# The product with C moved ahead of lane X's VectorE operations in the odd steps of a conv, state-space scan and attention kernel

## Chip, cores and metric

The kernel runs on one core of one Trainium2 chip. The metric is the device time of one execution in microseconds. The time before is the median of three runs, 5233.21 us (5232.01 to 5235.14).

## What is computed

The input is x, four images of 128 channels and 64 x 64 pixels, in fp32. Two layers follow each other. Layer 0 is a convolution block with a selective state-space scan ("mamba"); layer 1 is attention over the 4096 tokens of an image, followed by a mixture of eight experts of which each token takes two. Cut to what matters here:

```python
xn  = ln(group_norm(x));  y = xn + fc2(gelu(ln(conv3x3_depthwise(xn))))
u   = ln(y) split into 4 chunks of 32 channels           # each chunk is a sequence of 4096
xin = silu(conv1d(in_proj(u)));  z = silu(in_proj'(u))
dt, B, C = split(xin @ x_proj.T);  delta = softplus(dt @ dt_proj.T + b)
h_t = exp(delta_t * A) * h_(t-1) + delta_t * B_t * xin_t   # 64 channels x 16 states
y_t = sum over the 16 states of h_t * C_t                  # the product with C
m   = ((y + D * xin) * z) @ out_proj.T + chunks
t   = x + ln(xn + m) @ proj.T;  t = t + attention(ln(t));  out = t + experts(ln(t))
```

## The kernel before

**Work and tiles.** An image is cut into 8 blocks of 512 tokens, so there are 32 blocks (b, i). For a block the scan is done for two halves of the channels (p = 0, 1) and for the 16 states in pairs (n = 0, 2, ... 14): 512 units `(b, i, p, n)` in all (line 1299). The main loop (lines 1322 to 1373) gives each unit two steps of a counter `slot`, an even and an odd one, hence 1024 steps; a step takes some 4 to 5 us in the long middle of the run. Attention, the convolution block and the experts are threaded through the same steps.

**What a step issues, in this order.** `fetch` issues SyncE's load of the rows of B or C that a later unit needs (`rows`, a ring of 4 buffers); `prepared` has ScalarE make a decay `da` (and, in odd steps, copy the carried state into the next `h`). In an even step `driven` multiplies `h <- rows, du` on VectorE. Then `summed_up`, when a half block is done. Then `advance("X", True)`: the second half of lane X's current stage. Then `next(groups)` issues the score matmuls `sc` of attention on TensorE and `exponentials` two exponentials `pT <- sc` on ScalarE. In an even step `scan` follows on VectorE (`h <- da, state, h`, 1025 elements per partition), in an odd step `read`: the product with C, `hc <- rows, h`. Then come `advance("Y", False)`, the matmuls `y <- ident, hc` that TensorE uses to turn and sum the halves of an `hc`, `advance("Y", True)`, `kept` (ScalarE saves the state), the matmuls `av <- pT, v` of the group before, and last `advance("X", False)`.

**Order is fixed.** Every operation goes through `Queue` (lines 461 to 471), whose helper (line 467 in the profile, for all of them) ties it to the one before it on its engine. So each engine runs its operations in the order in which the Python code emits them, and only waits for others come on top.

**Lanes.** X and Y are two queues of stages, each written as a generator. A stage's first half (`advance(lane, False)`) mostly issues TensorE work into the lane's one PSUM tile (`ps_X`, `ps_Y`); its second half (`advance(lane, True)`, in the step after for lane X) reads that tile, mostly on VectorE. Lane Y prepares blocks (`first_norm`, `conv`, `inputs`). Lane X closes blocks (`closed`, line 848: the output projection, two layer norms, q, k and v) and, when the softmax sums of a pair of blocks are there, finishes them (`finished`, line 1087: router and experts).

**GpSimd in the layer norms.** `normalised` (line 545) takes mean and variance on VectorE (`st`, `mv`), then writes `rs` and `shift` there, and has GpSimd raise `rs` to the power -0.5 (`rs <- rs, mhalf`) and multiply `shift <- shift, rs`. One stage later ScalarE applies both (`xt`), ahead of that step's exponentials in ScalarE's queue.

**The product's own ties.** `hc` has two buffers, and is read by TensorE no sooner than the step after (`due`, lines 1348 to 1350: slot + 1 and slot + 2, two later when n is 0). It reads `h`, which the scan of the step before has written, and a `rows` buffer, which SyncE can fill again once the product is done.

Of the kernel before, what the change touches and what calls it, by code (L numbers as in the profile page):

```python
# [36 lines left out]
def conv_mamba_attn_moe_kernel(ctx: ExitStack, tc: tile.TileContext, t: dict):  # L37
# [448 lines left out]
    def flush():  # L486
        for entry in outgoing:
            entry[0] -= 1
            if entry[0] == 0:
                sync.dma_start(out=entry[1], in_=entry[2])  # L490
        outgoing[:] = [entry for entry in outgoing if entry[0]]
# [302 lines left out]
    def kept(unit, h):  # L794
        b, i, p, n = unit
        if i < NB - 1:
            scalar.copy(states[b % 2][:, p, n : n + 2], h[:, :, BLK - 1])

    def driven(unit, h, w):
        b, i, p, n = unit  # L800
        du = in_of[b, i, p][3]
        vector.tensor_mul(h[:, :, 0:BLK], w, du[:, None, :].to_broadcast([P, 2, BLK]))

    def scan(unit, h, da):

        b, i, p, n = unit
        h, da = (a.rearrange("p k q -> p (k q)")[:, 0 : 2 * BLK + 1] for a in (h, da))
        vector.tensor_tensor_scan(
            out=h, data0=da, data1=h, initial=states[b % 2][:, p, n : n + 1],
            op0=ALU.mult, op1=ALU.add,  # L810
        )

    def read(h, w):
        hc = mix.tile([P, 2, BLK], F32, name="hc", bufs=2)
        vector.tensor_mul(hc, w, h[:, :, 0:BLK])
        return hc
# [7 lines left out]
    def turned_on(y, term, first, last):  # L824

        for j in range(NT):
            s = slice(j * P, (j + 1) * P)
            tensor.matmul(
                y[:, s], lhsT=term[:, s], rhs=ident, start=first and j == 0,
                stop=last and j == NT - 1, is_transpose=True,  # L830
            )

    def summed_up(b, i, p, y):
        scanned(b, i, p, y)
        done.add(("scan", b, i, p))
        if p == 1:
            lanes["X"].appendleft((("closed", b, i), closed(b, i), []))

    def turned_back(b, i, p, yT):
        y = ps_y.tile([P, BLK], F32, name="y")  # L840
        for j in range(NT):
            tensor.transpose(y[:, j * P : (j + 1) * P], yT[:, j * P : (j + 1) * P], ident)
        return b, i, p, y
# [184 lines left out]
    def exponentials(group):  # L1028
        pTs = []
        for v, sc in group[3]:  # L1030
            pT = att.tile([P, 2, BLK], F32, name="pT", bufs=4)
            scalar.activation(pT, sc, AF.Exp, scale=ATT_SCALE)
            pTs.append((v, pT))
        return *group[:3], pTs, *group[4:]

    def weighted(group):
        b, q, h, pTs, first, last, prev, final = group
        if first:
            sums[0] = ps_av.tile([P, BLK], F32, name="av")
        av = sums[0]  # L1040
        for k, (v, pT) in enumerate(pTs):
            for u in range(2):
                mm(
                    av[64 * u : 64 * u + 2 * DH, :], v, pT[:, u, :],
                    first and k == 0, last and k == STEP - 1,
                )
        if last:
            avs = att.tile([P, BLK], F32, name="avs", bufs=2)
            if prev is None:
                scalar.copy(avs, av)  # L1050
            else:
                vector.tensor_add(avs, av, prev)


            if not final:
                partial[b, q, h] = dram.tile([P, BLK], F32, name=f"avd{q}{h}")
                send(partial[b, q, h], avs, 3)
                return
            if h == 0:
                total[b, q] = dram.tile([2, 2, NH, DH, BLK], F32, name=f"total{q}")  # L1060
            d = total[b, q]
            send(d[:, :, h].rearrange("u k r q -> (u k) r q"), avs, 3)
            if h == NH - 1:
                work_left = inverted(b, q)
                later.extend((slot + n, work_left) for n in (4, 6, 8))
# [150 lines left out]
    def advance(lane, second):  # L1216

        if inside[lane] != second:
            return False
        while True:  # L1220
            if lane not in running:

                tasks = lanes[lane] if lanes[lane] or slot < END else lanes["X"]
                if tasks and lane == "Y" and tasks[0][0][0] == "closed":
                    return False
                if not tasks or not all(k in done for k in tasks[0][2]):
                    return False

                if (
                    tasks[0][0][0] == "out" and slot < END + 4  # L1230
                    and not 2 <= slot % (2 * NST) < NST + 2
                ):
                    return False
                key, stages, _ = tasks.popleft()
                running[lane] = key, stages(lane) if callable(stages) else stages
            key, stages = running[lane]
            try:
                next(stages)
                inside[lane] = not second
                return True  # L1240
            except StopIteration:
                assert not second
                done.add(key)
                del running[lane]
# [57 lines left out]
    rows, due, closing, y_of = {}, deque(), deque(), {}  # L1302
    h_of, slot = {}, 0

    def fetch(*wanted):
        for ahead, k in wanted:
            if ahead < len(units):
                until(("in", *units[ahead][:3]))
                rows[ahead, k] = fetched(units[ahead], k)

    def prepared(ahead, k):
        if ahead < len(units):
            decayed(units[ahead], decays[ahead % 2], k)
            if k:
                h_of[ahead] = carried(units[ahead])

    def ends(unit):
        return unit[3] == NST - 2
# [3 lines left out]
    while (  # L1322
        slot < END or due or closing or summing or waiting or left or later or lanes["X"] or running
    ):
        at, odd = divmod(slot, 2)
        flush()
        if slot == 0:
            fetch((0, 0), (0, 1), (1, 0))
            prepared(0, 0)
            prepared(0, 1)  # L1330
        fetch((at + 2, 0) if odd else (at + 1, 1))
        unit = units[at] if at < len(units) else None
        prepared(at + 1, odd)
        if unit and not odd:
            h = h_of.pop(at)
            driven(unit, h, rows.pop((at, 0)))
        if summing:
            summed_up(*summing)
            summing = None
        advance("X", True)  # L1340
        group = next(groups, None)
        if group:
            group = exponentials(group)
        if unit and not odd:
            scan(unit, h, decays[at % 2])
        if unit and odd:
            hc = read(h, rows.pop((at, 1)))
            late = 2 * (unit[3] == 0)
            due.append((slot + 1 + late, unit, 0, hc[:, 0, :], False))
            due.append((slot + 2, unit, 1, hc[:, 1, :], ends(unit)))  # L1350
        advance("Y", False)
        while closing and closing[0][0] <= slot:
            summing = turned_back(*closing.popleft()[1:])
        while due and due[0][0] <= slot:
            _, (b, i, p, n), k, term, done_with = due.popleft()
            first = n == 0 and k == 0
            if first:
                y_of[b, i, p] = ps_y.tile([P, BLK], F32, name="y")
            turned_on(y_of[b, i, p], term, first, done_with)
            if done_with:  # L1360
                yT = mix.tile([P, BLK], F32, name="yT")
                scalar.copy(yT, y_of.pop((b, i, p)))
                closing.append((slot + 1, b, i, p, yT))
        advance("Y", True)
        if unit and odd:
            kept(unit, h)
        if waiting:
            weighted(waiting)
        waiting = group
        advance("X", False)  # L1370
        while later and later[0][0] <= slot:
            next(later.popleft()[1])
        slot += 1
# [113 lines left out]
```

## Time and profile before

| | |
|---|---|
| median of three runs | 5233.21 us |
| the profiled execution: its own time, its span | 5221.24 us, 5219.4 us |
| TensorE matmul (PE) busy, share of the span | 4743.5 us, 91% |
| VectorE (DVE) busy | 3834.5 us, 73% |
| ScalarE (ACT) busy | 3749.8 us, 72% |
| GpSimd (POOL) busy | 423.5 us, 8% |
| granted TensorE clock, mean | 0.958 of full speed |
| `hc` products: count, mean duration | 512, 1219 ns |
| scans: count, mean duration | 512, 2352 ns |

How to read it: times in the profile are microseconds unless they are marked ns. A group is a line, an engine, an operation and its tiles, out<-in, with the numbers of the buffers left out. "Idle before" is time in which the engine stood still just ahead of the operation, and the name after the arrow is what ended that wait. In the timeline each row is a start, a length, an engine, an operation, its shape and how many were merged; a bracket at its end holds the idle time ahead of it. Matmul ends are modelled, so a short stall of TensorE can hide in the length of the matmul before it. In the stretch from 0 to 600 us attention has little to do yet, and TensorE is busy for 370 of 600 us; from 600 to 4640 us it is busy for 95% of the time, beside the scan; what follows is attention and experts without a scan.

### The profile page before, as it was taken

Reading aid. Unit: us, or ns where it says so; the run is one execution under the profiler, and the core shown is the slowest. Engines: PE = TensorE matmul, PEld = TensorE weight load, DVE = VectorE, ACT = ScalarE, POOL = GpSimd, SP = SyncE. Lnnn points to the kernel's source line nnn. Section 1 sums busy time; section 2 is a strip of 40 time slices with the busy share of each in tenths; the row PEclk is TensorE's granted clock in tenths of the full one; section 3 lists DMA queues with packets and bytes.
Section 4 is the critical chain, followed back from the end, with each engine's and each line's share of the span. In section 5 each row is a group of like instructions: output and inputs, shape, how many; then the busy total and the mean of one; then the engine's idle time right before and its main releaser. Section 6 shows DMA issues by size and latency. Waiting matters only on the chain.

```text
span 5219.4 us, 62693 instructions
## 1 busy us (share of the span) xinstructions
PE 4743.5 (91%) x20704; PEld 2300.7 (44%) x20704; DVE 3834.5 (73%) x5809; ACT 3749.8 (72%) x5701; POOL 423.5 (8%) x483
## 2 busy tenths in 40 slices
PE   4566898999999999899999999999999999999997
PEld 2333444444444444444444444444444444443443
DVE  4888767777788877888788877888788877751332
ACT  3456787788777777688887787788777787756543
POOL 1111101100000000001000000000000001000000
PEclk8677999999999999899999999999999999999998
DMA  3556667767776667767766667767766666754542
GB/s 96 188 186 202 206 215 247 232 231 238 244 231 218 227 227 243 238 232 246 260 230 231 224 223 230 262 227 259 259 236 227 215 230 226 263 181 153 184 134 72
DMA packets 451694, 1131.62 MB, mean 217 GB/s; under 512 B 51985, under 2 KB 135330, under 8 KB 451362
## 3 DMA queue, kind: packets, MB, share of 16 engines
q1 hardware_dynamic: 450194, 1126.74, 64.3%
q8 instruction: 166, 2.72, 0.2%
q14 instruction: 166, 1.36, 0.1%
q10 hardware_dynamic: 1168, 0.80, 0.1%
HBM read 967.12 MB, written 143.39 MB: 213 GB/s over the span
## 4 chain that ended last, share of the span: by engine, by line
PE 55%; DVE 18%; ACT 13%; DMA 6%; issue 5%; POOL 2%; SPq 1%; DVEq 0%; ACTq 0%; POOLq 0%
PE av L467 23%; PE sc L467 13%; PE ps_X L467 8%; DVE h L467 6%; PE ps_Y L467 5%; PE y L467 5%; ACT pT L467 4%; ACT L467 3%; DMA ks<-kd 2%; DVE hc L467 2%; ACT xt L467 1%; ACT e L467 1%; DMA rows<-bcd 1%; DVE stX L467 1%; POOL rsX L467 1%
## 5 line engine op out<-in xcount | busy, mean ns | idle before, releaser
L467 ACT ACTIVATE pT<-sc 128x1024 f32<-128x1024 f32 x2048 | 1984.8, 1023 | 940.1 <-PE sc L467 938.4
L467 PE MATMUL av<-pT,v 128*64 128x512 f32 x8192 | 1998.3, 609 | 12.4 <-DVE avs L467 12.4
L467 PE MATMUL sc<-qs,ks 128*128 128x512 f32 x4096 | 1296.1, 436 | 64.4 <-DMA ks<-kd 32.7
L467 DVE TENSOR_TENSOR_SCAN h<-da,state,h 128x1025 f32<-128x1025 f32 x512 | 1204.2, 2352 | 90.0 <-ACT h L467 56.2
L467 PEld LDWEIGHTS sc<-qs,ks 128*128 128x128 f32 x4096 | 701.3, 190 | 793.3 <-ACT pT L467 261.7
L467 PEld LDWEIGHTS av<-pT,v 128*64 128x64 f32 x8192 | 499.5, 137 | 844.4 <-issue 813.8
L467 ACT ACTIVATE da<-delta,amat 128x512 f32<-128x512 f32 x1024 | 743.0, 730 | 1.9
L467 PE MATMUL y<-ident,hc 128*128 128x128 f32 x4096 | 626.6, 284 | 64.9 <-DVE hc L467 64.9
L467 DVE TENSOR_TENSOR hc<-rows,h 128x1024 f32<-128x1024 f32 x512 | 624.2, 1219 | 16.1 <-PE y L467 5.9
L467 DVE TENSOR_TENSOR h<-rows,du 128x1024 f32<-128x1024 f32 x512 | 623.4, 1218 | 14.2 <-DMA rows<-bcd 13.7
L467 PEld LDWEIGHTS y<-ident,hc 128*128 128x128 f32 x4096 | 520.6, 147 | 235.7 <-issue 83.9
L467 ACT ACT_TABLE_LOAD x319 | 409.3, 1283 | 19.5 <-DVE zs L467 14.3
L467 POOL TENSOR_TENSOR rsX<-rsX,mhalf 128x4 f32<-128x4 f32 x92 | 203.8, 2216 | 2524.6 <-DVE rsX L467 2440.5
L467 POOL TENSOR_TENSOR rsY<-rsY,mhalf 128x4 f32<-128x4 f32 x100 | 130.4, 1304 | 2071.0 <-DVE shiftY L467 1560.3
L467 DVE TENSOR_TENSOR avs<-av,prev 128x512 f32<-128x512 f32 x96 | 66.1, 689 | 252.9 <-PE av L467 238.3
L467 PE MATMUL ps_X<-share,w_ew 128*128 128x512 f32 x432 | 215.5, 622 | 8.7 <-DVE share L467 8.5
L467 ACT ACTIVATE xt<-ps_Y,shiftY,rsY 128x128 f32<-128x128 f32 x380 | 143.8, 469 | 106.4 <-POOL shiftY L467 99.0
L467 DVE TENSOR_TENSOR share<-share,xf 128x1024 f32<-128x1024 f32 x128 | 155.9, 1218 | 15.6 <-DMA share<-sharesX 9.9
L467 ACT COPY state<-h 128x2 f32<-128x2 f32 x448 | 88.7, 198 | 93.5 <-DVE h L467 93.5
L467 DVE SCALAR_TENSOR_TENSOR cm<-y,w_fc1w,cm 128x512 f32<-128x512 f32 x192 | 142.8, 744 | 3.4
L467 PE MATMUL ps_Y<-pairs,inxc 128*128 128x512 f32 x256 | 129.2, 629 | 15.6 <-DMA pairs<-xn 10.3
L467 PEld LDWEIGHTS ps_X<-share,w_ew 128*128 128x128 f32 x432 | 73.6, 190 | 146.8 <-issue 98.5
(254 smaller groups left out, 3455.8 us busy)
## 6 DMA issues: line engine op xcount, KB each, us to landing
rows<-bcd SPq DMA_DIRECT2D x1024, 512.0 KB
ks<-kd SPq DMA_DIRECT2D x192, 512.0 KB
qs<-qd SPq DMA_DIRECT2D x161, 512.0 KB
share<-sharesX SPq DMA_DIRECT2D x108, 512.0 KB
v<-vd SPq DMA_DIRECT2D x192, 256.0 KB
ks<-kd SPq DMA_DIRECT2D x128, 256.0 KB
avd<-avs SPq DMA_DIRECT2D x96, 256.0 KB
prev<-avd SPq DMA_DIRECT2D x96, 256.0 KB
```

The costliest lines, as they stand in the source:

```text
L467: return lambda *args, **kw: queued(op(*args, **kw))
```

## The change

In an odd step `read` is now called ahead of `advance("X", True)`, not after it and after the attention group:

```diff
         if summing:
             summed_up(*summing)
             summing = None
+        if unit and odd:
+            hc = read(h, rows.pop((at, 1)))
         advance("X", True)
         group = next(groups, None)
...
         if unit and odd:
-            hc = read(h, rows.pop((at, 1)))
             late = 2 * (unit[3] == 0)
             due.append((slot + 1 + late, unit, 0, hc[:, 0, :], False))
             due.append((slot + 2, unit, 1, hc[:, 1, :], ends(unit)))
```

Nothing is added or removed. Set side by side, the two programs have the same order on TensorE, ScalarE, GpSimd and SyncE. On VectorE the product passes lane X's operations in 247 of the 512 odd steps; in the other 265 lane X has nothing for VectorE there. What it passes, with the names that the prediction uses:

| step | what stands ahead of `hc` before, and behind it after | steps |
|---|---|---|
| A (`closed`) | `cm<-ps_X,cm`, `xr` | 31 |
| B (`closed`) | `tt<-ps_X,rsX,xr` (4), `stX` (4), `mvX` (4), `rsX`, `shiftX` | 31 |
| C (`closed`) | `hi`, `lo` of the queries, from `ps_X` | 31 |
| D (`finished`) | `acc<-ps_X,acc`, `stX` (4), `mvX` (4), `rsX` | 22 |
| E (`finished`) | `prX<-ps_X,rsX` and three small ones | 22 |
| F (`finished`) | 17 small ones from `top1X` to `bothX` | 22 |
| G (`finished`) | `res<-ps_X,xf` | 22 |
| H (`finished`) | `share<-share,xf` | 22 |
| I (`finished`) | `res<-res,ps_X`, `share<-share,xf` | 22 |
| J (`finished`) | `res<-res,ps_X` | 22 |

## The prediction

> **What bounds the kernel now.** I read first the page's busy times:
>
> ```profile
> PE 4743.5 (91%) x20704; PEld 2300.7 (44%) x20704; DVE 3834.5 (73%) x5809; ACT 3749.8 (72%) x5701; POOL 423.5 (8%) x483
> ```
>
> TensorE is the bound; by stretches it is busy for 3837 of the 4040 us from 600 to 4640, so there a change counts only through what TensorE waits for. Second, its waits in that stretch:
>
> ```profile
> PE ps_X L467 <- DVE bothX L467: 40.7, 21, 4.0
> PE sc L467 <- ACT pT L467: 28.0, 86, 1.6
> ...
> PE y L467 <- DVE hc L467: 13.2, 5, 6.7
> PE ps_Y L467 <- DVE gn L467: 13.1, 9, 2.1
> PE av L467 <- DVE avs L467: 12.4, 8, 2.9
> ```
>
> The product is hardly awaited (13.2 us, and most of that in steps that don't change), so having it sooner gains little by itself. Lane X's last result in step F, `bothX`, is awaited most, and in F the product now goes ahead of it. Third, the timeline of VectorE from D to F in one block:
>
> ```profile
> 1711.14 0.69 DVE L467 TENSOR_TENSOR acc<-ps_X,acc 128x512 f32<-128x512 f32 x1 [4.61 <-PE ps_X L467]
> ...
> 1713.13 1.22 DVE L467 TENSOR_TENSOR hc<-rows,h 128x1024 f32<-128x1024 f32 x1
> ...
> 1732.13 0.19 DVE L467 TENSOR_TENSOR bothX<-bothX,rsX 128x32 f32<-128x32 f32 x1
> 1732.24 1.22 DVE L467 TENSOR_TENSOR hc<-rows,h 128x1024 f32<-128x1024 f32 x1
> ```
>
> VectorE stands still for 4.61 us ahead of D's `acc`, then runs without a wait until `bothX` is done. Fourth, the timeline of all engines around a step B in the middle:
>
> ```profile
> 1641.58 1.12 DVE L467 SCALAR_TENSOR_TENSOR tt<-ps_X,rsX,xr 128x128 f32<-128x128 f32 x4 [0.86 <-PE ps_X L467]
> ...
> 1643.94 1.22 DVE L467 TENSOR_TENSOR hc<-rows,h 128x1024 f32<-128x1024 f32 x1
> 1644.04 1.98 POOL L467 TENSOR_TENSOR rsX<-rsX,mhalf 128x4 f32<-128x4 f32 x1 [1.96 <-DVE shiftX L467]
> ...
> 1645.08 1.22 DVE L467 TENSOR_TENSOR h<-rows,du 128x1024 f32<-128x1024 f32 x1
> ...
> 1646.11 0.25 POOL L467 TENSOR_TENSOR shiftX<-shiftX,rsX 128x4 f32<-128x4 f32 x1
> ...
> 1646.39 1.65 ACT L467 ACTIVATE xt<-tt,shiftX,rsX 128x128 f32<-128x128 f32 x4 [0.37 <-POOL shiftX L467]
> 1646.40 2.35 DVE L467 TENSOR_TENSOR_SCAN h<-da,state,h 128x1025 f32<-128x1025 f32 x1
> ...
> 1647.94 1.91 ACT L467 ACTIVATE pT<-sc 128x1024 f32<-128x1024 f32 x2
> ...
> 1649.90 0.73 PE L467 MATMUL sc<-qs,ks 128*128 128x512 f32 x2 [0.18 <-ACT pT L467]
> ```
>
> ScalarE waits for GpSimd's `shiftX`, its two `pT` come after `xt`, and TensorE's next `sc` starts 0.05 us after the second `pT` ends: here ScalarE is the bound, through GpSimd. Last, what GpSimd costs when VectorE's multiply and scan follow directly:
>
> ```profile
> 139.33 1.22 DVE L467 TENSOR_TENSOR h<-rows,du 128x1024 f32<-128x1024 f32 x1
> 139.43 1.98 POOL L467 TENSOR_TENSOR rsY<-rsY,mhalf 128x4 f32<-128x4 f32 x1 [17.44 <-DVE shiftY L467]
> ...
> 140.65 2.35 DVE L467 TENSOR_TENSOR_SCAN h<-da,state,h 128x1025 f32<-128x1025 f32 x1
> 141.49 1.51 POOL L467 TENSOR_TENSOR shiftY<-shiftY,rsY 128x4 f32<-128x4 f32 x1
> ```
>
> The multiply of 0.20 us (least of its group) takes 1.51 and ends when the scan does, at 143.00.
>
> [...] the power takes 1.01 us alone, 1.98 behind an `hc` or `h`, 2.98 behind a scan. [...] 0.78 granted before 600 us, 0.98 after. [...]
>
> **The change part by part.** One VectorE instruction moves in 247 steps; no DMA or other queue's order moves. Ends overlap starts by some 0.09 us, so a product shifts its neighbours by 1.13.
>
> *1. Steps with a wait ahead of lane X (most A, B, C, D, G): the product fills the wait.* VectorE then runs 1.13 us ahead until its next wait for another engine. `hc` is free to go: its scan is over, and its buffer was read by `y` matmuls that stand ahead of lane X's in TensorE's queue. Before 600 us VectorE is in the chain, and four blocks show the same two waits (3.6 to 4.8 us ahead of A, 0.83 ahead of B): 4 x (1.13 + 0.83) = 7.8 us gained. Five later blocks (near 717, 996, 1134, 1274, 2453) have TensorE waiting 0.52 us for A's successor `stX` and 2.1 for `gn` behind B: of these 2.6 up to 1.96 go, 5 x 1.96 = 9.8. Five waits for `avs` lose about 1.1 each, other single ones about 3: 8. Sum 25.6 us; none if something else is late next, such as `ks` loads (24.1 us awaited). What that leaves is 8 at least, the early part.
>
> *2. Step F and its sort (E, H, I): the product goes ahead of results that TensorE awaits.* By itself 1.13 x 22 = 25 us in F. But in 20 of 22 cases D waited over 1.2 us, and with no wait between D and F the lead of 1.13 us earned in D pays for F. The same lead, renewed in G, covers H and I. Left are F's two cases (2.3 us) and some H and I whose slack of 0.4 to 1.0 isn't covered, about 6: 8 us lost. If the lead didn't carry over, 25 + 17 (I) + 9 (H). Three costs I set at nothing: A's `cm` comes up to 1.13 later where its wait is short (about 0.6 us in most middle blocks), but the transposes that read it start 2.6 us or more after it there, behind the step's `av`; without that cover it would be some 0.6 x 20 = 12 us. C's `lo` waits for TensorE 2.7 to 3.4 us in most blocks, so the product fits; where it doesn't, up to 1.13 in 14 blocks. J feeds only a store, whose later start nobody awaits.
>
> *3. Step B: GpSimd's cover goes.* [...] After, `h` directly follows `shiftX` in the 15 blocks with no lane Y operation there. The power ends as before, 1.99 us after `shiftX`, but by then the scan is running: start 1.24, end 3.59. The multiply ends at 3.62, not 2.32: 1.30 later. Where B's wait is 0.86 us the product pushes `tt` by another 0.27. So `xt`, both `pT` and `sc` come 1.5 us later in 12 blocks, 2.4 in two without a wait, 1.3 in one with a long one: 18 + 4.8 + 1.3 = 24.1 us lost. In the others `gn`, `avs` or `du` stand between, and the power gets through sooner; that is worth nothing to 0.8 each, taken as nothing. ScalarE's slack could absorb some: bound 0 to 30.
>
> *4. SyncE.* `rows` loads wait for the product and block the queue behind them; they go sooner by lane X's 0.6 to 3.5 us. TensorE waits little for them: between 0 and 3 us gained, taken as 0.
>
> Sum: -25.6 + 8 + 24.1 = +6.5 us. On the profiled execution's own 5221.24 (span 5219.4 and 1.8 around it) that is 5227.7. It lies 12 us under the median of 5233.21; carried to the median, 5239.7.
>
> **Rivals.** *The port costs nothing* (faster): ScalarE or TensorE makes up the 24 us, because the multiply slips in ahead of the scan. For it: B's margin is under a microsecond. Against: `sc` follows `pT` by 0.05 us. -25.6 + 8 = -17.6: 5216 us. *The lead of D doesn't reach F* (slower): something between them, such as the scan's wait for `da`, takes it, and every `bothX` comes 1.13 later. For it: 40.7 us are awaited there already. Against: no wait is seen in the block above. It decides once half the F steps lose: +6.5 + 25 = +31.5: 5265 us. *The gains go elsewhere, the port cost stays* (slower): the second half of part 1 is given back to `ks` loads, or the new stalls bring half-clock windows: +24 + 8 - 8 = +24: 5257 us. The change surely does what it says, since the queue's order is fixed.
>
> **How the numbers follow.** The forecast, that gains and losses cancel to 5240, gets 0.42, all of it within 0.2% (10.5 us, about what a measurement here can tell from no change). Faster, with the first rival, 0.22. Slower: 0.20 for the lead, 0.16 for the port cost with gains lost: 0.36. The range of 8 in 10 reaches from just under the first rival's 5216 to the lead's 5265: 5213 to 5265.
>
> **What would show each step.** Part 1: `gn` and `stX` waits of TensorE near 996 to 1282 mostly gone; 600 us reached some 8 us sooner. Part 2: `bothX` still about 40 us awaited (over 60 if the lead fails). Part 3: the mean of GpSimd's `shiftX <- shiftX, rsX` rises, in some 15 blocks to 1.5 us, ending with the scan; ScalarE's wait for it rises from 63 to about 85 us, and TensorE's `sc <- pT` from 30 to over 50. I am wrong if `shiftX` doesn't lengthen, or if it does and `sc` doesn't follow.

## The result, and the profile after

The kernel after takes 5247.12 us (median of 22 runs, 5237.35 to 5254.91), the kernel before 5232.95 in as many runs beside it. The ratio is 1.0025, with a 95% interval of 1.0018 to 1.0033: some 13 us slower. The prediction said 5240, or +6.5 us. The sign of its sum holds and the time lies in its range, but the loss is twice as large and passes the 0.2% that its likeliest case was meant to stay within.

The profiled execution of after has a span of 5238.1 us and a time of its own of 5240.37. The one of before had 5219.4 and 5221.24, and stays 12 us under its median, so the two traces differ by more (18.7 us of span) than the kernels do. How much of that lies in the early part can be seen from three kernels of the experiments: with D to J, F or D early, the order on every engine is that of before up to the first D at 1337 us, and yet at 1300 us their TensorE is 5.6, 5.8 and 9.4 us behind that of the trace of before. So a gain read against that trace can come out 6 to 9 us too small by then.

The busy times on the page of after:

```profile
PE 4756.8 (91%) x20704; PEld 2312.5 (44%) x20704; DVE 3845.6 (73%) x5809; ACT 3749.2 (72%) x5701; POOL 456.7 (9%) x483
```

Nothing was added, and yet GpSimd is busy for 456.7 us, not 423.5: two of its groups are recorded as longer, `rsY <- rsY, mhalf` at 1800 ns in the mean (1304 before) and `shiftX <- shiftX, rsX` at 914 (460). TensorE's waits from 600 to 4660 us of after (us in total, times, longest):

```profile
PE ps_X L467 <- DVE bothX L467: 56.7, 21, 5.1
PE sc L467 <- ACT pT L467: 36.3, 100, 1.5
...
PE y L467 <- DVE hc L467: 9.3, 2, 6.7
...
PE av L467 <- DVE avs L467: 7.2, 5, 3.1
PE ps_Y L467 <- DVE gn L467: 4.5, 6, 0.8
```

`gn`, `avs` and `hc` are awaited 18 us less than before, `bothX` 16 us and `pT` 8 us more. The timeline of after from D to F in one block:

```profile
2730.63 1.23 DVE L467 TENSOR_TENSOR hc<-rows,h 128x1024 f32<-128x1024 f32 x1 [4.96 <-PE y L467]
2734.03 0.69 DVE L467 TENSOR_TENSOR acc<-ps_X,acc 128x512 f32<-128x512 f32 x1 [2.17 <-PE ps_X L467]
...
2750.82 1.22 DVE L467 TENSOR_TENSOR hc<-rows,h 128x1024 f32<-128x1024 f32 x1
...
2755.36 0.19 DVE L467 TENSOR_TENSOR bothX<-bothX,rsX 128x32 f32<-128x32 f32 x1
```

And the same block before:

```profile
2732.15 0.69 DVE L467 TENSOR_TENSOR acc<-ps_X,acc 128x512 f32<-128x512 f32 x1 [8.49 <-PE ps_X L467]
...
2734.13 1.22 DVE L467 TENSOR_TENSOR hc<-rows,h 128x1024 f32<-128x1024 f32 x1
...
2752.93 0.19 DVE L467 TENSOR_TENSOR bothX<-bothX,rsX 128x32 f32<-128x32 f32 x1
```

In D the product now waits for TensorE's `y` (a wait that the prediction had ruled out), but `acc` still waits 2.17 us after it, so this costs nothing. `bothX` starts 21.33 us after `acc`, against 20.78 before; in most of the 22 cases the difference is 0.2 us, where a product takes 1.13: the product in F is paid for, all but this, by the one that left the way in D. And the timeline of after around a B:

```profile
1634.78 1.22 DVE L467 TENSOR_TENSOR hc<-rows,h 128x1024 f32<-128x1024 f32 x1
...
1638.20 0.16 DVE L467 TENSOR_SCALAR shiftX<-mvX 128x4 f32<-128x4 f32 x1
1638.28 1.22 DVE L467 TENSOR_TENSOR h<-rows,du 128x1024 f32<-128x1024 f32 x1
1638.38 1.98 POOL L467 TENSOR_TENSOR rsX<-rsX,mhalf 128x4 f32<-128x4 f32 x1 [1.23 <-DVE shiftX L467]
...
1639.60 2.35 DVE L467 TENSOR_TENSOR_SCAN h<-da,state,h 128x1025 f32<-128x1025 f32 x1
...
1640.44 1.51 POOL L467 TENSOR_TENSOR shiftX<-shiftX,rsX 128x4 f32<-128x4 f32 x1
...
1641.98 1.65 ACT L467 ACTIVATE xt<-tt,shiftX,rsX 128x128 f32<-128x128 f32 x4 [1.82 <-POOL shiftX L467]
...
1643.53 1.91 ACT L467 ACTIVATE pT<-sc 128x1024 f32<-128x1024 f32 x2
...
1644.59 0.73 PE L467 MATMUL sc<-qs,ks 128*128 128x512 f32 x2 [0.58 <-ACT pT L467]
```

This is the stall that Part 3 forecast, in the block that the prediction shows of before: the power ends inside the scan, the multiply takes 1.51 us and ends with the scan (1641.95), ScalarE waits 1.82 us where it waited 0.37, and TensorE waits for `pT` behind it.

**Where TensorE loses and gains.** TensorE runs the same 20704 instructions in the same order in both kernels, so their starts can be set side by side. Taken at the matmuls `y` of each unit, and over the two units around each B: in the 15 blocks with no lane Y operation behind B, TensorE falls back by 23.5 us in sum (1.3 to 1.5 in twelve, 2.4 and 3.4 in two, 0.6 in one). In the other 16 it gains 18.3. Over the three units from D to F of the 22 cases it falls back by 9.3. Together +14.5 of the 18.7 us. Windows of five units around each B, which hold step C too, give the same 23.5 for the 15, but 25.8 for the other 16: that gain depends on where the windows end.

### The profile page after: what moved, and what is told of

The parts are those of the page before. It is cut to its first block, busy times and chain, and to the rows that moved or that the text cites. A ratio compares the mean times of both kernels' runs of the same rounds, so it can differ in the third digit from the quotient of the medians.

```text
span 5238.1 us, 62759 instructions
## 1 busy us (share of the span) xinstructions
PE 4756.8 (91%) x20704; PEld 2312.5 (44%) x20704; DVE 3845.6 (73%) x5809; ACT 3749.2 (72%) x5701; POOL 456.7 (9%) x483
## 5 line engine op out<-in xcount | busy, mean ns | idle before, releaser
L467 PE MATMUL sc<-qs,ks 128*128 128x512 f32 x4096 | 1301.7, 438 | 71.9 <-ACT pT L467 38.9
L467 PE MATMUL y<-ident,hc 128*128 128x128 f32 x4096 | 627.5, 285 | 56.7 <-DVE hc L467 56.7
L467 POOL TENSOR_TENSOR rsX<-rsX,mhalf 128x4 f32<-128x4 f32 x92 | 173.7, 1888 | 2508.2 <-DVE rsX L467 2430.2
L467 POOL TENSOR_TENSOR rsY<-rsY,mhalf 128x4 f32<-128x4 f32 x100 | 180.0, 1800 | 2074.1 <-DVE shiftY L467 1563.7
```

Of the source, the lines that this page charges most:

```text
L467: return lambda *args, **kw: queued(op(*args, **kw))
```

## The experiments

Most kernels below set the product early in some of the steps A to J only. A stage notes its letter ahead of the `yield` before its VectorE half, and the loop asks for it; the kernel after is `"ABCDEFGHIJ"`, the one before `""`:

```diff
+        early = kind.pop("X", "-") in EARLY
-        if unit and odd:
+        if unit and odd and early:
             hc = read(h, rows.pop((at, 1)))
         advance("X", True)
...
         if unit and odd:
+            if not early:
+                hc = read(h, rows.pop((at, 1)))
             late = 2 * (unit[3] == 0)
```

Each was timed beside the kernel before. My theory was that B's lock-out costs 24 us and F little, since D's lead pays for it. The rival was that the lock-out is made up and F carries the loss.

### B left out, and B alone

```diff
-    EARLY = "ABCDEFGHIJ"
+    EARLY = "ACDEFGHIJ"
```

> The kernel after, with the product left behind lane X in the 31 steps B alone. Theory (GpSimd's shift is locked out by the scan in B, 24 us): against the kernel before it comes to +13 - 24 + about 4 of B's own gain that goes too, so some -7 us (ratio 0.9987), and GpSimd's shiftX multiply in steps B is short again. Rival (the lock-out is seen in the trace but ScalarE and TensorE make it up; the loss is in F, where TensorE waits 16 us longer for bothX): as the kernel after or a little over it, +13 to +17 us (1.0025 to 1.0032).

Measured: 1.0004 (0.9996 to 1.0013), 5237.99 against 5238.39 us: 11 us less than the kernel after's ratio. The rival's 1.0025 is out, and so is the theory's 0.9987: B costs, but not a net 20 us.

```diff
-    EARLY = "ABCDEFGHIJ"
+    EARLY = "B"
```

> The kernel before, with the product ahead of lane X in the 31 steps B alone. Theory: +24 us from 15 steps with a locked-out multiply, less about 4 of B's own gain: +20 us (1.0038). Rival (the lock-out is made up): -4 to 0 us (0.9992 to 1.0).

Measured: 1.0009 (1.0000 to 1.0019), some +5 us: between the two, nearer to the rival. Its trace tells why: around B the same 15 blocks lose 28 us, and the other 16 gain some 15, a net +12.5. B's price was right, or a little low, and its own gain, set at about 4, was set too low.

### The shift without GpSimd's multiply

```diff
-        vector.tensor_scalar_mul(shift, mv[:, :, 0], -1.0)
+        if lane == "Y" or not closing_up:
+            vector.tensor_scalar_mul(shift, mv[:, :, 0], -1.0)
         gpsimd.tensor_tensor(rs, rs, mhalf, ALU.pow)
-        gpsimd.tensor_mul(shift, shift, rs)
+        if lane == "Y" or not closing_up:
+            gpsimd.tensor_mul(shift, shift, rs)
+        else:
+            shifts.append((shift, mv, rs))
...
             driven(unit, h, rows.pop((at, 0)))
+        if shifts:
+            shift, mv, rs = shifts.pop()
+            vector.scalar_tensor_tensor(shift, mv[:, :, 0], -1.0, rs, ALU.mult, ALU.mult)
```

> The kernel after, with lane X's shift = -mean * rs in the 32 closing blocks computed by one VectorE instruction right behind the next even step's h, instead of by GpSimd's multiply (and without VectorE's negation). The result is the same, and VectorE now waits some 0.8 us for GpSimd's power ahead of it. Theory [...]: xt is released some 2.2 us after the moments instead, and the kernel loses the price of B: 8 to 20 us below the kernel after, so -7 to +5 us against before (0.9987 to 1.001). Rival (B costs because the product itself delays the moments, not through GpSimd): as the kernel after, +13 us (1.0025).

Measured: 0.9990 (0.9983 to 0.9996), 5233.12 against 5239.41 us: 18 us below the kernel after's ratio, by moving one operation of 0.2 us. The timeline of this kernel behind the B of the same block:

```profile
1631.15 0.17 DVE L467 TENSOR_SCALAR rsX<-mvX 128x4 f32<-128x4 f32 x1
1631.23 1.23 DVE L467 TENSOR_TENSOR h<-rows,du 128x1024 f32<-128x1024 f32 x1
1631.40 1.92 POOL L467 TENSOR_TENSOR rsX<-rsX,mhalf 128x4 f32<-128x4 f32 x1 [1.24 <-DVE rsX L467]
...
1633.36 0.16 DVE L467 SCALAR_TENSOR_TENSOR shiftX<-mvX,rsX 128x4 f32<-128x4 f32 x1 [0.90 <-POOL rsX L467]
1633.44 2.35 DVE L467 TENSOR_TENSOR_SCAN h<-da,state,h 128x1025 f32<-128x1025 f32 x1
1633.56 1.65 ACT L467 ACTIVATE xt<-tt,shiftX,rsX 128x128 f32<-128x128 f32 x4 [0.38 <-DVE shiftX L467]
```

VectorE waits 0.90 us for the power and computes the shift ahead of the scan. ScalarE's wait is 0.38 us again, and the windows around B sum to -12.5 us where after had +5.2: 17.7 us, as the times say. The 15 blocks alone go from 23.5 us to 1.0, so the gain is where the multiply was locked out and not elsewhere. The product still goes ahead of the moments, so the rival is out: the lock-out is the cause of B's loss.

### D to J together, F alone, D alone

```diff
-    EARLY = "ABCDEFGHIJ"
+    EARLY = "DEFGHIJ"
```

> The kernel before, with the product ahead of lane X in the steps of the finishing stages (D to J) alone. Theory (the lead from D pays for F all but some tenths of a us, other small losses in F, H and I): +4 to +8 us (1.0008 to 1.0015). Rival (F carries the loss: the 16 us by which TensorE waits longer for bothX are the change's cost): +16 us (1.0031). If the lead failed wholly: +25 us or more (1.0048).

Measured: 1.0020 (1.0012 to 1.0028), +10.5 us.

```diff
-    EARLY = "ABCDEFGHIJ"
+    EARLY = "F"
```

> The kernel before, with the product ahead of lane X in the 22 steps F alone, so that no lead from D pays for it. Theory of the lead: bothX comes 1.13 us later in 22 steps and TensorE waits for it already, so about +23 us (1.0044), and the wait for bothX goes from 40 to over 60 us. Rival (TensorE's wait for bothX has slack behind it, or the lead from D counts for nothing): the same as in the kernel with D to J together, +4 to +16 us (1.0008 to 1.0031).

Measured: 1.0057 (1.0039 to 1.0076), +30 us. TensorE's waits from 600 to 4660 us of this kernel:

```profile
PE ps_X L467 <- DVE bothX L467: 65.6, 22, 5.2
```

```diff
-    EARLY = "ABCDEFGHIJ"
+    EARLY = "D"
```

> The kernel before, with the product ahead of lane X in the 22 steps D alone, where VectorE waits 1 to 5 us ahead of acc. Theory of the lead: VectorE is 1.13 us ahead from D on, and F, which keeps its old order, hands it on: bothX comes up to 1.13 us sooner and TensorE's wait for it falls from 40 to about 25 us, so some -12 us (0.9977). Rival (the lead is spent on the way from D to F, at the wait of the product for TensorE's y or at the scan): no change, -2 to +2 us (1.0).

Measured: 0.9934 (0.9921 to 0.9948), 5205.37 against 5239.41 us: -34 us, well beyond the theory's -12. The same wait in this kernel:

```profile
PE ps_X L467 <- DVE bothX L467: 32.8, 21, 4.0
```

From the start of `acc` to the end of `bothX` it takes 21.36 us in the mean before, 22.54 with F alone, 20.21 with D alone, 21.46 after. So the lead of D reaches F whole (1.15 us), and F spends it whole. The kernel after gains little from D because it moves F too.

### A and C, and the steps with long waits

```diff
-    EARLY = "ABCDEFGHIJ"
+    EARLY = "AC"
```

> The kernel before, with the product ahead of lane X in steps A and C alone. Theory (the product fills waits, and the gain is mostly the part before 600 us): -4 to -10 us (0.9981 to 0.9992). Rival (what A gives is taken back in the same block, because a decay or a load of rows is late next): -2 to +2 us (1.0).

Measured: 0.9977 (0.9966 to 0.9988), -12 us, a little more than the theory's.

```diff
-    EARLY = "ABCDEFGHIJ"
+    EARLY = "ACDG"
```

> The kernel before, with the product ahead of lane X in A, C, D and G alone, the steps where VectorE waits longer than the product takes in most cases; B, E, F, H, I and J as before. Theory: the gains of A, C and D add up and neither F's nor B's price is paid: -15 to -20 us (0.9962 to 0.9971). Rival (gains are taken back): -2 to +2 us (1.0).

Measured: 0.9905 (0.9890 to 0.9920), 5190.53 against 5239.41 us: -49 us, two and a half to three times the theory's, and about the -12 of A and C and the -34 of D together. A version faster than both kernels, by moving the product only where VectorE mostly has to wait anyway.

```diff
-    EARLY = "ABCDEFGHIJ"
+    EARLY = "ABCDG"
```

(with the shift on VectorE, as above)

> The kernel with the product early in A, B, C, D and G (E, F, H, I and J as before), and lane X's shift computed by one VectorE instruction behind the next even step's h, as in the run with that change on the kernel after. Theory (B early is a gain once the multiply is not locked out: the moments of B start up to 0.9 us sooner or at the same time, and xt is released 2.2 us after them instead of 2.3): -50 to -58 us against before (0.989 to 0.9905). Rival (VectorE's new wait for GpSimd's power takes what B gains): -42 to -48 us (0.991 to 0.992).

Measured: 0.9906 (0.9892 to 0.9921), 5185.30 against 5233.51 us: as with A, C, D and G, so B early brings nothing that could be measured, even with its lock-out gone. The interval of some 8 us each way holds both forecasts, so this decides neither.

### E, H, I and J

```diff
-    EARLY = "ABCDEFGHIJ"
+    EARLY = "ACDEGHIJ"
```

> The kernel after, with the product left behind lane X in B and F alone (A, C, D, E, G, H, I and J stay early). Theory (B and F carry the whole loss; E, H, I and J cost TensorE nearly nothing, since TensorE's progress in those steps is unchanged to 0.2 us): as the kernel with A, C, D and G, some -40 to -48 us against before (0.991 to 0.992). Rival (E, H, I and J cost, because the scan comes 0.4 us later in each of H, I and the step after J): -20 to -28 us (0.9946 to 0.9962).

Measured: 0.9941 (0.9928 to 0.9953), -31 us: 19 us above A, C, D and G alone, give or take 10. Neither fits; it is nearer to the rival.

```diff
-    EARLY = "ABCDEFGHIJ"
+    EARLY = "ACDGHI"
```

> The kernel with the product early in A, C, D, G, H and I; B, E, F and J as before. The kernel with E and J early too came to 0.9941 of the time before, the one with A, C, D and G alone to 0.9905. Theory (H and I carry the difference: TensorE waits 4 us longer for share, and is 0.2 us later in H of most blocks): 0.994, some -31 us. Rival (E and J carry it, by the scan that comes later behind them): 0.9905, some -48 us.

Measured: 0.9927 (0.9913 to 0.9940), -38 us, between the two. About 12 us would go to H and I and 7 to E and J, but the intervals overlap with both neighbours': how the 19 us are shared stays open.

### The clock behind F's wait

In F of D to J together `bothX` ends only 0.2 us later after `acc` and TensorE waits some 0.5 us longer for it, and still TensorE loses 1.3 us there. Two answers for the windows of time around that F of one block show why (PEclk, after POOL, is the granted share of TensorE's clock). With D to J early:

```profile
2764.00:2767.50 3.50, 1.40 (x8) 0.24 (x4) 3.02 (x17) 2.54 (x7) 1.71 (x5) 1.00 0.51 123
2767.50:2770.70 3.20, 2.73 (x9) 2.02 (x10) 3.06 (x4) 1.61 (x3) 0.00 (x0) 0.50 0.97 354
```

And before, in the same block:

```profile
2750.00:2753.10 3.10, 1.12 (x6) 0.14 (x2) 2.65 (x16) 2.49 (x7) 1.07 (x5) 1.00 0.00 0
2753.10:2756.30 3.20, 3.13 (x20) 2.23 (x22) 3.10 (x4) 2.52 (x5) 0.00 (x0) 1.00 0.20 54
```

The first row holds TensorE's wait (2.57 us, 2.06 before; with D to J early its last 0.47 us fall into the second row), the second what follows: the clock is halved for these 3.2 us, and 9 matmuls fall in them where 20 did. From the transposes of `bothX` to the product with `w_eb` it takes 5.6 to 5.8 us with one such stretch, not 4.2. To price this, F alone with its wait filled:

```diff
         ps = work(lane)
+        if lane == "X":
+            for _ in range(3):
+                mm(ps, ident, xf)
         for j in range(NT):
             tensor.transpose(ps[0 : 2 * NE, j * P : (j + 1) * P], both[:, j, :], ident)
```

> The kernel with the product early in F alone, and three matmuls of 128x512 more ahead of lane X's transposes of bothX; what they write is overwritten or never read, so the result is the same. They lie in the 3.2 us in which TensorE waits there. Theory (after a wait of 3.2 us TensorE runs a 3.4 us stretch at half clock in nearly every F, which costs about as much again as the 1.13 us of the wait; with the wait filled to 1.4 us the clock stays up): the half-clock stretches in F fall from 15 to 5 or fewer, and the time from +30 to about +8 us over before (1.0015). Rival (the cost of F is the later bothX alone, and the clock only goes along): +30 us as without them, or a little more (1.0057 or more).

Measured: 1.0051 (1.0035 to 1.0066), +27 us against +30 without the matmuls. The half-clock stretches in F fell from 15 to 1, and the way from the transposes of `bothX` to the product with `w_eb` from 5.39 to 4.31 us in the mean, as the theory said, but the time hardly followed: the intervals overlap, and the theory's 1.0015 is out. Most of F's price is the later `bothX` itself. The profiled execution with the matmuls is 14.7 us shorter than the one without (5254.91 and 5269.58), and the matmuls put the transposes off by 0.2 us in the mean; what the clock costs in time stays open between 0 and some 15 us.

## Why the prediction was right or wrong

- **Part 3, the lock-out** (24.1 us): right, in its 15 blocks, in its shape (the multiply ends 3.58 us after VectorE's `shiftX` in all 15, 3.62 forecast) and in size (23.5). Behind the scan the multiply is recorded at 1.51 us, against 0.20 at its shortest, and both end together (1641.95 above). The run with the shift on VectorE shows this as the cause: without GpSimd's multiply the 15 blocks lose 1.0 us. What the prediction calls the cost of the port is this lengthening; what it comes from inside the chip, no run shows. The rival in which it costs nothing is out.
- **Part 1, the filled waits** (-25.6 us): the mechanism is right, and no run shows its size wrong. The gain is 18.3 us in the windows of two units around the 16 other B, 25.8 in those of five. A and C by themselves are timed at -12, and B's own part in the run with B alone is some 15. The early part looks short against the trace of before, 2 us gained by 600 us and 7 by 1300, where Part 1 had 8 and 16. Against the three traces whose order is that of before until then it is 3.2 to 7.8 us by 600 and 12.9 to 16.8 by 1300: near the forecast.
- **Part 2, the lead of D**: right that it carries to F (20.21, 22.54 and 21.46 us). What failed is "the same lead, renewed in G, covers H and I": E, H, I and J cost 19 us, not some 6. (The 19 is uncertain by 10.) In the total of D to J, forecast at +8 and measured at +10.5, this doesn't show, perhaps because D alone gives -34 and F alone costs +30, so -4 where the sum left +2.3 (the intervals are 7 and 10 us wide each way). That the total came out so near was in part luck.
- **The 6.6 us between +6.5 and +13**: which term was short is not shown. Timed apart, A and C (-12), B (+5) and D to J (+10.5) add up to +3.5, and the intervals of these and of the whole, 4 to 6 us each way, only just allow +13.
- **What was not in the sum**: the halved clock behind waits that grew from 2.1 to 2.6 us. Windows of half clock stood only in a rival. In the profiles, 5 of the 22 F steps of before have one, 9 of after, 13 of D to J. But the kernel with A and C alone, whose F is that of before, has 12: the number varies from one execution to the next, and that the change raises it is not shown.
- **What would show**: `gn` fell from 13.1 to 4.5 us and `stX` from 5.0 to 2.4. `bothX` was to stay at 40 us, and more than 60 was to mean a failed lead; it reached 56.7, with the lead intact. The total of a wait was a poor sign: the interval from `acc` to `bothX` was the right one. ScalarE's wait for `shiftX` rose from 63.3 to 69.4 us, not 85: in the 15 blocks it rose by the 22 us forecast (from 6.2 to 28.9), but elsewhere it fell by 17. TensorE's wait for `pT` rose from 30.5 to 38.9 over the whole execution, not over 50: behind a stall TensorE shows waits of 0.58 and 0.17 us, where one of 0.18 stood before, and falls back by 1.4; the rest seems to hide in modelled matmul ends.

The result lies between the forecast and the rival of 5257, in which the 24 us of Part 3 stay and the gains go elsewhere or half-clock windows come up. The 24 us stayed whole (23.5 measured); the windows do come up (9 of 22 F steps, 5 before); that the gains of Part 1 went elsewhere is not shown.

## What to carry to other kernels

An early start of a long operation was cheap here where its engine would have stood still, and the lead earned there was worth most where nothing downstream spent it: the same edit cost 13 us in all steps and saved 49 in the four kinds where VectorE mostly waits. Two profiled executions of the same order can be 5 to 9 us apart (here by 1300 us), so a gain of that size is read against more than one trace of before. Before moving an operation away from between two others, ask which operation of another engine ran beside it: here GpSimd's multiply came to lie beside the scan, and went from 0.25 to 1.51 us. A wait of the bounding engine is best judged by the interval that feeds it, not by its total.

## What the runs showed of the hardware

**Half clock after waits of 2 us and more.** Over the 14 profiles of this case, the F steps by the length of TensorE's wait for `bothX` (to the nearest tenth), and in how many the clock was halved within 3 us of it:

| wait, us | under 2.0 | 2.0 to 2.2 | 2.3 to 2.9 | 3.0 to 3.5 | 3.6 and more |
|---|---|---|---|---|---|
| halved | 0 of 150 | 18 of 42 | 35 of 62 | 11 of 12 | 42 of 42 |

In each of the 14 traces, the changes of the clock fall on one grid of 3.41 us (to 0.01). From 600 to 4640 us, 201 of the 312 half-clock stretches that start there last one step of it and 62 two. A wait need not fill a whole step to be followed by such a stretch (over 2.05 us in one step were, 102 of 102). What tells the halved F steps from the others is the longest part of the wait that lies inside one step of the grid:

| part of the wait inside one step, us | under 1.9 | 1.9 to 2.05 | over 2.05 |
|---|---|---|---|
| halved | 0 of 190 | 4 of 16 | 102 of 102 |

So some 2.05 us without a matmul, 60% of a step, were enough, if they fell into one step. A wait of the same 2.1 us is hit in 2 of 11 F steps of before and in 8 of 12 of the kernel with A and C: by the table, it is hit when a border of the grid doesn't cut it. (Matmul ends are modelled, so a true idle time can be longer than the wait shown.) In the four sets of runs of the kernel before (38, 27, 11 and 9), a longer time goes with a lower granted clock (correlation -0.59 to -0.84). That fits, but doesn't show which causes which.

**GpSimd pays in its own durations.** An operation of 0.20 us was recorded at 1.51, with no wait shown ahead of it. Here the lock-out is seen in the mean of a group, not in its waits: `shiftX <- shiftX, rsX` went from 460 to 914 ns and `rsY <- rsY, mhalf` from 1304 to 1800, while `rsX <- rsX, mhalf`, which in after took under 1.2 us in 37 of 92 cases instead of 8, fell from 2216 to 1888.
